# Four graph layers on one core: filler products on TensorE, one transposition bank, 512-wide work on gathered tiles, and a different first graph

## Chip, core and metric

The kernel runs on one core of a Trainium2 chip. Five engines work side by side, each through its own instructions in a fixed order: TensorE (PE; its weight loads are listed apart as PEld), VectorE (DVE), ScalarE (ACT), GpSimd (POOL) and SyncE (SP, which only issues transfers). The metric is the device time of one execution in microseconds; the number quoted for a kernel is the median of several runs.

## What is computed

Sixteen graphs of 1024 nodes with 64 features each pass through four layers. Every layer normalises the features, cuts them at zero, applies a graph operation and adds the result to its input.

```python
h = jnp.maximum(_layernorm(x, axis=-1), 0.0)
x = x + _L0_gnn_ref(h, adj, L0_gnn_W)        # adj @ h, then @ W.T
h = jnp.maximum(_layernorm(x, axis=-1), 0.0)
x = x + _L1_gnn_ref(h, adj, ...)             # two dense layers, adj @ m, a GRU cell
h = jnp.maximum(_layernorm(x, axis=-1), 0.0)
x = x + _L2_gnn_ref(h, adj, ...)             # Chebyshev: k0*h + k1*(A h) + k2*(2 A(A h) - h), @ weight
h = jnp.maximum(_layernorm(x, axis=-1), 0.0)
x = x + _L3_gnn_ref(h, adj, nodemask, ...)   # per node: quantiles over its kept neighbours, then an MLP
```

`adj` is dense in storage (1024 x 1024 float32 per graph, 4 MB) but has about nine non-zero entries in a row. The first three layers use it as a matrix. The last one needs, for each node, the list of its neighbours (with some of them dropped by a rule on the count), then for each of the 64 features the weighted sum of the 0.25, 0.5 and 0.75 quantiles over that list, a two-layer MLP and the node mask.

## The kernel before

**One program, seven chains.** The class `Fast` writes the work down as Python generators, each yielding operations one after another: `transposing` (load a graph's adjacency in eight blocks of 128 columns, 512 KB each, transpose them on PE, copy them out of PSUM by ACT into `AT` tiles), `coding` (from the signs of `AT`, bit codes of each node's neighbours, by small PE products), `listing` (from the codes, each node's list of up to 24 neighbours, on DVE), two `layering` chains (layers 0 to 2 and the last norm; one takes the even graphs, the other the odd ones), `gathering` (POOL fetches the neighbours' feature rows from a table in DRAM by indirect transfers of 128 rows each) and `quantiling` (sorting networks on DVE over the gathered rows; then `dense`, the weighting, the MLP and the output).

**The order is reckoned beforehand.** `Weave.run` takes the chains' next operations, gives each a cost from `Line.cost`, reckons when it could start, and fixes one order for each engine: earliest start first, within `SLACK` the chain with the lowest key. Keys put graph b's layers (b - 3) ahead of its transposing (b - 2.5), coding (b - 2), listing (b - 1.5), and gathering and sorting (b + 1). On the chip each engine runs its own order and waits where data are not there yet. So a wrong cost in `Line.cost` doesn't change what an instruction takes; it changes the order. Nearly all instructions are recorded at L301, in `Line`'s helper, and so are told apart by tile names.

**Buffers.** A chain asks for a tile by the name of its stock and blocks until one has been given back. Those that matter here: `pay` (4 tiles: a graph's features, its list and its notes, held from the load of x until its output is stored), `G` (2 tiles: gathered rows, 11 slots of 8 node tiles, 66 columns each), `net` (1 tile: the second buffer of the sorting network), `nodes` (3), `AT` (15), and the eight PSUM banks: two for transpositions (`tp`), one for codes (`bits`), two for `q` (quantiles, MLP and a few others), three for the layers (`fm`). Waits between engines go by regions of a tile: a gather into slot 2 of a G tile waits only for the readers of slot 2.

**Graph 0.** `layers` loads x, then for each of three layers normalises (`norm`) and multiplies by the `AT` tiles as they come. In `norm`, ACT makes the squares in eight pieces with an accumulated sum each, and eight relus with a scale; each relu is followed by what the caller passes as `then` (a pair of products per `AT` tile, or a transposition). At the end the graph's list and the normalised features are put into `pay`, and SP stores them to the tables from which POOL gathers.

**After gathering.** `quantiles` marks dropped neighbours with 1e30, runs the network `NETWORKS[11]` (28 minimum or maximum steps on 1 to 5 slots each), and weights the sorted slots. A step on k slots is cut by `parts(k)` into instructions of at most `few` slots, where `few` comes from `LONGEST` elements; a slot of a graph has 512. The nodes with more neighbours than these slots hold are gathered again at the end, in nine tiles (`MANY`), and their outputs are scattered over the earlier ones.

Of the kernel before, what the change touches and what calls it, by code (L numbers as in the profile page):

```python
# [16 lines left out]
AF = mybir.ActivationFunctionType  # L17
ALU = mybir.AluOpType
AX = mybir.AxisListType
# [3 lines left out]
P = 128  # L23
N = 1024
NT = N // P
C = 64
NB = 64
S = N // NB
# [18 lines left out]
SELF, COUNT, IDX, H, DROPS, MASK, TO, XS, W = ROW  # L47
# [57 lines left out]
LONGEST = 1024  # L105
# [180 lines left out]
class Line:  # L286
# [17 lines left out]
    def cost(self, method, out, reads, kwargs):  # L304
        n = max(a.free_size() for a in [out] + reads)
        extra = "accum_out" in kwargs
        if self.name == "DVE":
            fixed = {"match_replace": 0.27, "max": 0.16}.get(method, 0.155)
            return fixed + n / 960 + 0.08 * extra, 0.0
        if self.name == "ACT":  # L310
            scalars = sum(hasattr(kwargs.get(k), "ap") for k in ("bias", "scale"))
            return 0.225 + n / 1400 + 0.09 * scalars + 0.19 * extra, 0.0
        if self.name == "PE":
            if method == "transpose":
                return 0.12, 0.25
            n = out.free_size()
            if n == NB and mybir.dt.size(reads[0].dtype) == 2:
                return 0.12, 0.3
            pair = n == 512 and reads[0].shape[0] == P and out.shape[0] == C
            return (0.46 if pair else max(0.22, 0.06 + n / 545)), 0.3  # L320
        if self.name == "SP":
            return 0.4, 2.0 + out.nbytes() / 150e3
        return 1.33, 2.2


class Weave:
# [6 lines left out]
    def __init__(self, tc):  # L333
        self.tc = tc
        self.free, self.past, self.last, self.stocks, self.chains = {}, {}, {}, {}, []
        self.ends, self.time, self.free_pairs, self.count = {}, 0.0, set(), 0
        self.leash = None
        self.awaited, self.made = [], {}
# [4 lines left out]
    def give(self, name, t):  # L343
        self.stocks[name].append(t)
# [13 lines left out]
    def of_others(self, op, line):  # L358

        found = []  # L360
        for mine, kinds in ((op.reads, "w"), (op.writes, "wr")):
            for name, lo, hi, p0, p1 in mine:
                for (l, h, q0, q1, kind, other), made in self.made.get(name, {}).items():
                    if other is line and kind in kinds and l < hi and lo < h and q0 < p1 and p0 < q1:
                        found.append(made)
        return [max(found, key=lambda f: f[:2])] if found else []

    def note(self, op, start, ins):
        end = start + op.cost
        self.count += 1  # L370
        for mine, kind in ((op.reads, "r"), (op.writes, "w")):
            for name, lo, hi, p0, p1 in mine:
                past, made = self.past.setdefault(name, {}), self.made.setdefault(name, {})
                if kind == "w":
                    for e in [e for e in past if lo <= e[0] and e[1] <= hi and p0 <= e[2] and e[3] <= p1]:
                        del past[e], made[e]
                past[lo, hi, p0, p1, kind, op.line] = end + op.later
                made[lo, hi, p0, p1, kind, op.line] = end, self.count, ins
# [27 lines left out]
    def issue(self, op, start, of):  # L406

        line, ins = op.line, op.make()
        if line is self.leash[0]:


            done = [i for end, _, i in self.awaited if end <= start]
            self.awaited = self.awaited[len(done):]
            if done:
                self.after(ins, done[-1])
        self.free[line] = start + op.cost
        self.time = max(self.time, start + op.cost)
        if line is not self.leash[1]:
            self.awaited = sorted(self.awaited + self.of_others(op, self.leash[1]), key=lambda a: a[:2])
        self.note(op, start, ins)  # L420
        self.ends[ins.ins.name] = start + op.cost + op.later
        free = False
        for other in self.last.get(line, ()):
            self.behind(ins, other)
        if line in self.last:
            free = (ins.ins.name, self.last[line][0].ins.name) in self.free_pairs
        self.last[line] = [ins] + (self.last[line] if free else [])
        return ins

# [36 lines left out]
class Fast:  # L466
# [4 lines left out]
    def __init__(self, tc, half, whole, weights):  # L471
        self.tc, self.nc = tc, tc.nc
        (W0, W1, b1, W2, b2, Wih, bih, Whh, bhh, Wc, K, bc, M1, mb1, M2, mb2) = weights
        nc = self.nc
# [92 lines left out]
        self.G, self.D = Line("POOL", nc.gpsimd), Line("SP", nc.sync)  # L567
        self.take = {}
        weave.leash = None, None
# [5 lines left out]
        self.bank = banks[0]  # L575
        weave.stock("tp", banks[0:2])
# [58 lines left out]
    def listing(self, nodemask):  # L635
        V = self.V
        mf, mu8 = self.small("h1", (P, 512))[:, 0:P], self.small("h1")[:, P:2 * P].bitcast(U8)[:, 0:P]
        yield self.D.dma_start(mu8, nodemask.rearrange("b (t p) -> (b t) p", p=P))
        yield V.tensor_copy(mf, mu8)
        bank = yield "q"  # L640
        yield self.T.transpose(bank[:, 0:P], mf, self.ident)
        self.mask = self.small("mask", (P, P))
        yield V.tensor_copy(self.mask, bank[:, 0:P])
        self.weave.give("q", bank)
        for b in range(GRAPHS):
            yield float(b) + LIST_KEY
            yield from self.lists(b)
        yield float(GRAPHS) - RANK
        yield from self.longest()

    def coding(self):

        V, T, S = self.V, self.T, self.S
        for b in range(GRAPHS):
            yield float(b) + CODE_KEY
            bank = yield "bits"
# [188 lines left out]
    def transposing(self, adj):  # L845
# [5 lines left out]
        early = self.early  # L851

        def load(i):
            b, j = divmod(i, NT)
            blocks[i] = block = early.pop(0).rearrange("p (t m) -> p t m", m=P) if 2 <= i < NT else (yield "block")
            yield D.dma_start(block, adj[b, :, j * P:(j + 1) * P].rearrange("(t p) m -> p t m", p=P))
# [22 lines left out]
    def norm(self, w, h, X, then=None):  # L879
# [4 lines left out]
        yield V.tensor_scalar(st, st, -1.0 / C, None, op0=ALU.mult)  # L884
        sq = self.small(f"sq{w}", (P, C))
# [10 lines left out]
    def layers(self, w, b, x):  # L896
# [36 lines left out]
        yield from self.norm(w, h, X, into(bank, h))  # L933
# [25 lines left out]
        yield from self.norm(w, h, X, turn)  # L959
# [63 lines left out]
        yield from self.norm(w, h, X, into(bank, h))  # L1023
# [27 lines left out]
        aug = yield "wide"  # L1051
        for half in range(2):
            yield S.activation(aug[0:C, cols[half]], both[half * C:(half + 1) * C, :], AF.Copy)
        give("fm", both)
        bank = yield "fm"
        o = yield from by_node(bank, aug[0:C, :], self.wca, self.bcr)
        give("wide", aug)
        yield V.tensor_add(X, X, o)
        give("fm", bank)

# [12 lines left out]
        yield from self.norm(w, pay[:, :, H:H + C], X)  # L1073
# [873 lines left out]
```

## Time and profile before

| | |
|---|---|
| median of 9 runs | 2264.45 us (2258.52 to 2275.44) |
| the profiled execution | 2274.12 us, span 2272.3 us |
| mean granted clock of PE | 0.757 |
| first gather issued / last gather issued | 161.0 / 2227.9 us |
| graph tables stored by SP (graphs 0, 1, 2, 3, 4) | 155.7, 255.7, 372.9, 476.5, 594.1 us |
| PE, DVE, ACT, POOL busy from 300 to 1700 us | 1186.7, 1041.3, 810.5, 1045.1 of 1400 us |
| granted clock of PE from 300 to 1700 us | 0.80 |
| adjacency block, SP to landing | 512 KB, 4.5 us |

The profile is of one execution. An engine's busy time is the union of its instructions. A row such as `DVE G L301 ... x97 | 117.5, 1221 | 1.0` gives a group of like instructions: count, busy us together, mean ns of one, and idle time ahead of them. In a timeline row the first two numbers are start and length in us, and the bracket gives how long the engine stood idle just before and which work ended that. In a row of waits, "A <- B: total, times, longest" says how long A stood until B released it. The granted clock is the share of its full clock that PE was given; the trace knows only the values 1 and 0.5, and a stretch's number is their mean.

### The profile page before, as it was taken

Reading aid. Unit: us, or ns where it says so; the run is one execution under the profiler, and the core shown is the slowest. Engines: PE = TensorE matmul, PEld = TensorE weight load, DVE = VectorE, ACT = ScalarE, POOL = GpSimd, SP = SyncE. Lnnn points to the kernel's source line nnn. Section 1 sums busy time; section 2 is a strip of 40 time slices with the busy share of each in tenths; the row PEclk is TensorE's granted clock in tenths of the full one; section 3 lists DMA queues with packets and bytes.
Section 4 is the critical chain, followed back from the end, with each engine's and each line's share of the span. In section 5 each row is a group of like instructions: output and inputs, shape, how many; then the busy total and the mean of one; then the engine's idle time right before and its main releaser. Section 6 shows DMA issues by size and latency. Waiting matters only on the chain. (4 is left out here: it accounts for less than half of the span.)

```text
span 2272.3 us, 24102 instructions
## 1 busy us (share of the span) xinstructions
PE 1662.2 (73%) x7024; PEld 762.7 (34%) x7024; DVE 1551.6 (68%) x3675; ACT 1095.3 (48%) x3002; POOL 1570.6 (69%) x1441
## 2 busy tenths in 40 slices
PE   5869697888887888797988897888888762332303
PEld 2333333343434343343343343343333321111302
DVE  1515277695968695958687867777776889939745
ACT  4555546564756565656565646465555531011000
POOL 2017776777777787777677777576777677877773
PEclk9778788868887878787888778787768675555555
DMA  4123434352636252535243434344252413121110
GB/s 115 47 53 83 75 79 75 64 93 44 93 73 94 53 94 53 77 69 79 58 80 68 67 63 76 66 77 69 53 78 62 35 30 36 27 29 24 33 26 11
DMA packets 246841, 141.00 MB, mean 62 GB/s; under 512 B 76048, under 2 KB 223952, under 8 KB 246704
## 3 DMA queue, kind: packets, MB, share of 16 engines
q0 software_dynamic: 46096, 48.62, 18.5%
q1 hardware_dynamic: 199824, 90.21, 16.4%
q8 instruction: 59, 0.97, 0.2%
q10 hardware_dynamic: 784, 0.57, 0.1%
q14 instruction: 78, 0.64, 0.1%
HBM read 120.12 MB, written 19.17 MB: 61 GB/s over the span
## 5 line engine op out<-in xcount | busy, mean ns | idle before, releaser
L622 POOL DMA_INDIRECT G<-table,pay x1402 | 1538.8, 1098 | 655.3 <-issue 337.6
L301 PE MATMUL bank<-AT,nodes 128*64 128x512 f32 x2048 | 621.7, 691 | 48.1 <-ACT nodes L301 23.2
L301 PE MATMUL bank<-G,c 128*128 128x512 f32 (+3 forms) x382 | 190.0, 617 | 169.7 <-DVE G L301 169.7
L301 PEld LDWEIGHTS bank<-AT,nodes 128*64 128x64 f32 x2048 | 162.4, 155 | 358.5 <-issue 235.9
L301 PE MATMUL bank<-c,block 128*128 128x128 f32 x976 | 215.4, 347 | 35.3 <-DMA block<-in_adj 28.4
L301 ACT ACTIVATE sq<-pay,st 128x64 f32<-128x64 f32 x512 | 177.7, 347 | 96.4 <-DVE st L301 82.5
L301 ACT ACTIVATE AT<-bank 128x512 f32<-128x512 f32 x256 | 150.5, 589 | 121.5 <-PE bank L301 120.4
L301 PEld LDWEIGHTS bank<-c,block 128*128 128x128 f32 x976 | 142.2, 176 | 171.9 <-issue 125.0
L301 DVE TENSOR_TENSOR G<-G 128x1024 f32<-128x1024 f32 (+7 forms) x215 | 187.5, 903 | 2.2
L301 ACT ACTIVATE nodes<-pay,off,ri 128x64 f32<-128x64 f32 x384 | 153.6, 429 | 23.1 <-DVE off L301 22.8
L301 ACT ACTIVATE wide<-bank 64x512 f32<-64x512 f32 x128 | 75.7, 591 | 180.6 <-PE bank L301 179.6
L301 PEld LDWEIGHTS bank<-G,c 128*128 128x128 f32 x382 | 69.5, 226 | 275.7 <-issue 142.7
L301 ACT ACTIVATE G<-G,coef 128x64 f32<-128x64 f32 x384 | 95.2, 336 | 128.0 <-DVE coef L301 128.0
L301 DVE TENSOR_TENSOR net<-G 128x1024 f32<-128x1024 f32 (+7 forms) x140 | 140.5, 1033 | 3.1 <-PE bank L301 2.0
L301 ACT ACTIVATE there<-AT 128x1024 f16<-128x1024 f32 x128 | 132.4, 1045 | 0.3
L301 PE MATMUL bank<-c,nodes 128*64 128x128 f32 x128 | 50.8, 400 | 86.3 <-ACT nodes L301 85.9
L301 DVE TENSOR_TENSOR G<-net 128x512 f32<-128x512 f32 (+12 forms) x123 | 109.4, 938 | 1.4
L301 DVE TENSOR_TENSOR G<-G,net 128x1024 f32<-128x1024 f32 (+5 forms) x113 | 104.3, 960 | 1.4
L301 DVE SCALAR_TENSOR_TENSOR G<-bad,G 128x1024 f32<-128x1024 f32 (+3 forms) x89 | 102.6, 1202 | 0.0
L301 PE MATMUL bank<-wide,wg 64*64 64x512 f32 (+1 forms) x192 | 101.4, 609 | 1.1 <-ACT wide L301 1.0
L301 DVE MAX8 L<-cand 128x8 f16<-128x103 f16 x384 | 92.3, 263 | 8.8
L301 DVE TENSOR_TENSOR more<-more,top 128x64 f32<-128x64 f32 x80 | 17.7, 221 | 116.4 <-ACT sq L301 116.4
(188 smaller groups left out, 2375.1 us busy)
## 6 DMA issues: line engine op xcount, KB each, us to landing
block<-in_adj SPq DMA_DIRECT2D x122, 512.0 KB, 4.5
G<-table,pay POOLq DMA_INDIRECT x1402, 2.7
rows<-pay SPq DMA_DIRECT2D x16, 632.0 KB, 9.6
table<-pay SPq DMA_DIRECT2D x16, 264.0 KB, 5.0
pay<-in_x SPq DMA_DIRECT2D x16, 256.0 KB, 4.1
out<-yo SPq DMA_DIRECT2D x16, 256.0 KB, 2.8
G<-in_adj SPq DMA_DIRECT2D x6, 512.0 KB, 9.7
c<-in_half ACTq DMA_DIRECT2D x1, 246.0 KB, 7.7
```

The lines of the kernel that those rows point to most:

```text
L301: return Op(self, lambda: f(*args, **kwargs), writes, reads, cost, later)
L622: return self.nc.gpsimd.indirect_dma_start(out=out, out_offset=None, in_=table, in_offset=bass.IndirectOffsetOnAxis(ap=at, axis=0))
```

## The change

- **Fillers.** `Weave.fill`: before an operation of PE is placed, the gap that the reckoned order leaves ahead of it is taken. If it is over 0.22 us and layers are still being placed, and the reckoned PE work of the last 3.4 us is under half of that, products of a constant (`ones16`, 128 x 512 float16) are put in front, for at most 0.7 of the gap at 0.22 us each. They write a bank that nobody reads.
- **Banks.** That bank is the first of the two that were in `tp`; one is left for transpositions.
- **Costs.** `Line.cost` has other costs for PE (a half of a pair of 512 columns 0.27 in place of 0.46, others to match, a small f16 product 0.05 in place of 0.12), for DVE's `match_replace` and `max`, and one for transfers on any queue.
- **Width.** `LONGEST` is 512 in place of 1024: at most one slot of a graph in an instruction.
- **First graph.** The first blocks' loads with odd number go through ACT's queue, the others through SP's. The node mask is cast and transposed only once graph 0's codes are there. Coding starts when graph 0's first aggregation is through. Graph 0's norms make the squares and the scaled relu on DVE over all eight pieces at once.
- **All graphs.** At the end of `layers` the list and the notes are put into `pay` ahead of the last product with the weights, not behind it.
- **Taken out.** The code around `leash`, which was set to `None, None`.

```diff
-LONGEST = 1024
+LONGEST = 512
+WINDOW = 3.4
+DENSITY = 0.5
+SPARE = 0.7
+FILL = 0.22
...
     def cost(self, method, out, reads, kwargs):
+        if method == "dma_start":
+            return 0.4, 2.0 + out.nbytes() / 150e3
...
-            fixed = {"match_replace": 0.27, "max": 0.16}.get(method, 0.155)
+            fixed = {"match_replace": 0.145, "max": 0.155}.get(method, 0.155)
...
             if method == "transpose":
-                return 0.12, 0.25
+                return 0.125, 0.25
             n = out.free_size()
             if n == NB and mybir.dt.size(reads[0].dtype) == 2:
-                return 0.12, 0.3
+                return 0.05, 0.3
             pair = n == 512 and reads[0].shape[0] == P and out.shape[0] == C
-            return (0.46 if pair else max(0.22, 0.06 + n / 545)), 0.3
-        if self.name == "SP":
-            return 0.4, 2.0 + out.nbytes() / 150e3
+            return (0.27 if pair else max(0.15, 0.06 + n / 1100)), 0.3
         return 1.33, 2.2
...
     def issue(self, op, start, of):
-        line, ins = op.line, op.make()
-        if line is self.leash[0]:
...
+        line = op.line
+        if line is self.filled:
+            self.fill(start, op.cost)
+        ins = op.make()
...
+    def fill(self, start, cost):
+        line = self.filled
+        gap = start - self.free.get(line, 0.0)
+        self.recent = [(a, c) for a, c in self.recent if a > start - WINDOW]
+        if gap > FILL and any(c["gen"].__name__ == "layering" for c in self.chains):
+            lacking = DENSITY * WINDOW - sum(c for _, c in self.recent)
+            for _ in range(int(min(lacking, SPARE * gap) / FILL)):
+                ins = self.filler()
+                for other in self.last.get(line, ()):
+                    self.behind(ins, other)
+                self.last[line] = [ins]
+                self.recent.append((start, FILL))
+        self.recent.append((start, cost))
...
-        self.bank = banks[0]
-        weave.stock("tp", banks[0:2])
+        self.bank = spare = banks[0]
+        weave.filler = lambda: nc.tensor.matmul(spare, self.ones16[:, 0:P], self.ones16, start=True, stop=True)
+        weave.stock("tp", banks[1:2])
...
         yield self.D.dma_start(mu8, nodemask.rearrange("b (t p) -> (b t) p", p=P))
+        yield lambda: 0 in self.coded
         yield V.tensor_copy(mf, mu8)
...
             yield float(b) + CODE_KEY
+            yield lambda: self.turns > 0
             bank = yield "bits"
...
-            yield D.dma_start(block, adj[b, :, j * P:(j + 1) * P].rearrange("(t p) m -> p t m", p=P))
+            queue = self.A if i % 2 and i < NT else D
+            yield queue.dma_start(block, adj[b, :, j * P:(j + 1) * P].rearrange("(t p) m -> p t m", p=P))
...
-    def norm(self, w, h, X, then=None):
+    def norm(self, w, h, X, then=None, early=False):
...
+        if early:
+            yield V.tensor_add(h, X, st[:, :, None].to_broadcast([P, NT, C]))
+            square = yield "nodes"
+            yield V.tensor_mul(square, h, h)
+            yield V.tensor_reduce(va, square, axis=AX.X, op=ALU.add)
+            self.weave.give("nodes", square)
+            yield S.activation(sd, va, AF.Sqrt, bias=self.eps, scale=1.0 / C)
+            yield V.reciprocal(ri, sd)
+            yield V.scalar_tensor_tensor(h, h, 0.0, ri[:, :, None].to_broadcast([P, NT, C]), op0=ALU.max, op1=ALU.mult)
+            for t in range(NT):
+                if then:
+                    yield from then(t)
+            return
...
-        yield from self.norm(w, pay[:, :, H:H + C], X)
+        yield from self.norm(w, pay[:, :, H:H + C], X, early=b == 0)
```

More of the change, by code (lines that the diff above doesn't have):

```diff
@@ L335, in __init__ @@
         self.free, self.past, self.last, self.stocks, self.chains = {}, {}, {}, {}, []
-        self.ends, self.time, self.free_pairs, self.count = {}, 0.0, set(), 0
-        self.leash = None
-        self.awaited, self.made = [], {}
+        self.ends, self.time, self.free_pairs = {}, 0.0, set()
+        self.filled, self.recent = None, []
     def stock(self, name, tiles):
@@ L356, in ready, with note @@
         return t
[L358 to L368, printed above, removed]
+    def note(self, op, start):
         end = start + op.cost
-        self.count += 1
         for mine, kind in ((op.reads, "r"), (op.writes, "w")):
             for name, lo, hi, p0, p1 in mine:
-                past, made = self.past.setdefault(name, {}), self.made.setdefault(name, {})
+                past = self.past.setdefault(name, {})
                 if kind == "w":
                     for e in [e for e in past if lo <= e[0] and e[1] <= hi and p0 <= e[2] and e[3] <= p1]:
-                        del past[e], made[e]
+                        del past[e]
                 past[lo, hi, p0, p1, kind, op.line] = end + op.later
-                made[lo, hi, p0, p1, kind, op.line] = end, self.count, ins
     def advance(self, chain):
@@ L406, in issue @@
     def issue(self, op, start, of):
-        line, ins = op.line, op.make()
-        if line is self.leash[0]:
[L412 to L415, printed above, removed]
+        line = op.line
+        if line is self.filled:
+            self.fill(start, op.cost)
+        ins = op.make()
         self.free[line] = start + op.cost
         self.time = max(self.time, start + op.cost)
-        if line is not self.leash[1]:
-            self.awaited = sorted(self.awaited + self.of_others(op, self.leash[1]), key=lambda a: a[:2])
-        self.note(op, start, ins)
+        self.note(op, start)
         self.ends[ins.ins.name] = start + op.cost + op.later
@@ L567, in __init__ @@
         self.G, self.D = Line("POOL", nc.gpsimd), Line("SP", nc.sync)
+        self.A = self.S
         self.take = {}
-        weave.leash = None, None
+        weave.filled = self.T
         def stock(name, count, shape, dtype=F32):
@@ L932, in layers @@
         bank = yield "fm"
-        yield from self.norm(w, h, X, into(bank, h))
+        yield from self.norm(w, h, X, into(bank, h), early=b == 0)
         self.turns += 1
@@ L958, in turn @@
                 give("fm", turned_h[-1])
-        yield from self.norm(w, h, X, turn)
+        yield from self.norm(w, h, X, turn, early=b == 0)
         aug = yield "wide"
@@ L1022, in layers @@
         bank = yield "fm"
-        yield from self.norm(w, h, X, into(bank, h))
+        yield from self.norm(w, h, X, into(bank, h), early=b == 0)
         wide = yield "wide"
@@ L1050, in layers @@
         give("nodes", h)
[L1051 to L1059, printed above, removed]
         yield lambda: b in self.listed
@@ L1072, in layers @@
         give("notes", notes)
-        yield from self.norm(w, pay[:, :, H:H + C], X)
+        aug = yield "wide"
+        for half in range(2):
+            yield S.activation(aug[0:C, cols[half]], both[half * C:(half + 1) * C, :], AF.Copy)
+        give("fm", both)
+        bank = yield "fm"
+        o = yield from by_node(bank, aug[0:C, :], self.wca, self.bcr)
+        give("wide", aug)
+        yield V.tensor_add(X, X, o)
+        give("fm", bank)
+        yield from self.norm(w, pay[:, :, H:H + C], X, early=b == 0)
         table = self.table[b * STRIDE:b * STRIDE + N, :].rearrange("(t p) c -> p t c", p=P)
```

## The prediction

> **What bounds the kernel now.** I read the page's engine totals first, then the gathers by tile.
>
> ```profile
> PE 1662.2 (73%) x7024; PEld 762.7 (34%) x7024; DVE 1551.6 (68%) x3675; ACT 1095.3 (48%) x3002; POOL 1570.6 (69%) x1441
> PEclk9778788868887878787888778787768675555555
> ...
> POOL G L622 <- DMA table<-pay: 145.1, 2, 143.6
> ...
> L622 POOL DMA_INDIRECT G<-table,pay x1402: 938/945/1997, 161.0 to 2227.9; - x176
> ```
>
> No engine is full by its share, yet POOL (GpSimd) sets the time. It waits 143.6 us for the first table, gathers from 161.0 to 2227.9, and hardly stops. The 1402 gathers, 9 row gathers and 9 scatters are busy 1538.8 + 10.8 + 9.3 = 1558.9 us. The pauses after 161.0 are 655.3 + 2.7 + 30.1 - 143.6 = 544.5 us: in the instruction records, 1419 of them with a median of 0.305 (433 us) plus 112 us beyond that in 22 long ones, of which 27 lie between the last scatters. So 161.0 + 1558.9 + 544.5 = 2264.4, and some 8 us follow. Three terms can shrink: the 161 us ahead, the time that gathers lose above their floor of 0.945 (1558.9 - 1420 x 0.945 = 217 us), and about 85 us of long pauses inside the loop.
>
> The second term comes from DVE (VectorE):
>
> ```profile
> 1069.39 1.98 POOL L622 DMA_INDIRECT G<-table,pay  x1 [0.30 <-ACT nodes L301]
> ...
> 1069.34 1.22 DVE L301 TENSOR_TENSOR net<-G,net 128x1024 f32<-128x1024 f32 x1
> 1070.59 1.23 DVE L301 TENSOR_TENSOR net<-G 128x1024 f32<-128x1024 f32 x1
> ```
>
> The gather took 1.98 us beside two 1.22 us operations on the sorting tiles. Over all records, the 257 gathers that met no DVE instruction average 0.944; the 411 that mostly met a 1024-wide G or net operation average 1.347 (+0.403, 166 us together); the 108 that met a 512-wide one 1.126 (+0.182).
>
> The third term: graph b+2's gathers need the G buffer that graph b's sort still reads.
>
> ```profile
> 1099.39 0.96 POOL L622 DMA_INDIRECT G<-table,pay  x1 [11.26 <-PE bank L301]
> ...
> 1097.83 0.23 DVE L301 TENSOR_TENSOR more<-more,top 128x64 f32<-128x64 f32 x1 [10.63 <-ACT sq L301]
> ...
> 428.86 0.38 SPq L628 DMA_DIRECT2D out<-yo  x1
> 429.30 0.58 SPq L301 DMA_DIRECT2D pay<-in_x  x1
> ```
>
> While POOL waits 11.26, DVE itself stands 10.63 in its fixed order behind an ACT (ScalarE) read. Sorting starts 13 to 51 us after its gathers end (graphs 1 to 14), though DVE idles 18 to 41 us per graph through graph 12. The last two lines show the pay ring: graph 4's x is loaded when graph 0's output leaves. From graph 3 to graph 13 the period is (1673.3 - 496.5) / 10 = 117.7 us, of which 80 x (0.944 + 0.305 + 0.15 lost) = 112 is gathering.
>
> **First graph (the 161 us).**
>
> ```profile
> 23.80 0.23 DVE L301 CAST h<-h 128x128 f32<-128x128 uint8 x1 [11.18 <-DMA h<-in_nodemask]
> 24.08 0.18 PEld L301 LDWEIGHTS bank<-c,h 128*128 128x128 f32 x1 [10.10 <-DVE h L301]
> 25.23 0.44 ACT L301 ACTIVATE nodes<-pay,off,ri 128x64 f32<-128x64 f32 x1 [10.21 <-DVE off L301]
> ```
>
> The node mask is queued on SP behind eight 512 KB loads, and DVE, PE (TensorE) and ACT all stand about 10 us behind its cast. The change makes cast and transposition wait for the first code. Transposing then runs from 13.3, where block 0 is there. With one bank, four transpositions (0.66), the ACT copy (0.60) and two hand-overs (some 0.2) follow each other: 1.46 a half, 1.6 with the product that does not fit under the copy; 16 halves end at 13.3 + 25.6 = 39, the last pair at 40 in place of 51: -11. The DMA engines are full from 8 to 22 us (268 to 302 GB/s), so the second queue moves that end little. Four loads on ACT hold it 4 x 2.3 us (SP's median there) from 5.3 to 14.5, just when the first copy is due; at 3.6 each, 5 us are lost. The weights that PE's set-up awaits until 11.6 were issued ahead of them. Range -14 to -6.
>
> Norms of graph 0: before, 8 x 0.47 of squares on ACT, then 8 relus between products. After: four 512-wide DVE operations (four by 0.69), root 0.30, reciprocal 0.20, gaps 0.2, that is 3.5. Second norm with its transpositions: from 16.6 us (51.0 to 67.6) to about 10.2, counting copy 1.2, product 2.0, add 0.7, sums 0.9, 3.5, eight transpositions 1.3, copy 0.6: -6.4. Third: 6.8 to 4.4, and relus no longer between the products: -5.4. Last: 144.4 to 155.6 becomes 4.6: -6.6. Together -18.4. Pay's six small DVE operations (143.69 to 144.41) go under PE's products: -0.7. Coding (8 copies of 1.045 on ACT, 128 small products) now follows the first aggregation instead of lying in it, and returns +4. Half-clock products between 67 and 79 (four in 3.67 us, against about 0.6 each at full clock) shrink by 4 if fillers hold the clock, 0 if not. Sum -30, bounds -42 to -12. POOL gets it all only if tables 1 and 2 (stored at 255.7 and 372.9, POOL then waited 1.5 and 11.6) move as far; I take **-28**.
>
> **Width 512.** Per graph the network has 66 slot operations: 40 instructions before, 66 after; mask adds 5, weighting 3: 34 more. Over all, 555 operations of 1.22 become 1110 of 0.686 (+84 us DVE, 5.1 a graph), hidden under the idle above. If that cover is gone, it goes into the G wait in full, +84. Gathers that meet them: 411 x 1.12 = 461; at +0.182 they lose 84 in place of 166 (-82), at a loss proportional to length (+0.226) 104 (-62), at an unchanged +0.403, +20. I take **-65**, near the proportional end, range -82 to +20.
>
> The Trainium skill (SBUF — State Buffer, "Who interferes with whom") speaks against this: a two-input DVE operation blocks only a GpSimd instruction that reads SBUF, and descriptor writing is inferred untouched. By it, if descriptor writing is what these gathers do, width would gain 0; by the rows, 65. The rows decide.
>
> **New costs, order, fillers.** The modelled cost of a 128x512 pair half goes from 0.46 to 0.27. Measured: 621.7 / 2048 = 0.30 busy each, so 0.27 is nearer; DVE's and ACT's places in the order shift everywhere. No row prices that. Bounds: all long loop pauses vanish (-85), or DVE's stalls stay and the 84 above appears. I take **-25**, a third: the dearest stall, "more" behind "sq", is 109.8 us in 300 to 1700, and PE would be faster. The clock there is 0.80, so 40% of the time is at half. Fillers (0.22 each modelled) can be at most 15% idle x 117.7 x 0.7 / 0.22 = 56 a graph. They wait for nothing; behind one stand only PE's own products, delayed by 0.22 to 0.44. Recovering half of the lost clock takes about 11% off PE's 1187 us there.
>
> The skill (TensorE: Matmul & The Clock Gate, "What's actually happening") says the clock halves after an idle window of about 3.4 us. Here spans at half clock last up to 65 us although PE is 81% busy in those of the loop; so half a window of density need not hold it. By the rule all -4 and more would come; by the row perhaps none.
>
> One bank fewer: 16 hand-overs of 0.7 a graph, 0 to 11 us of PE, taken as 2 and covered by the 24 us between graph 4's table (594.0) and its first gather (618.1). The deleted leash code matches no engine: 0. Tail: two or three more 0.15 us operations, 0.3.
>
> **Sum.** 2274.1 (the profiled execution's own time; span 2272.3) - 28 - 65 - 25 = 2156. It ran 9.7 above the median of 2264.45, so the forecast is **2146**, own range 2090 to 2200.
>
> **Rivals.**
> *DVE takes it back.* The sort of b must end before b+2's second slot is gathered; cheaper gathers only wait longer. For: sorting always starts late. Against: DVE idles. Then only the first graph counts: 2264 - 28 = 2236.
> *POOL runs free.* Pauses gone, shorter meeting, -30 - 75 - 75: 2084. For: DVE and PE have idle time; against: in-order queues never lost all of it.
> *Nothing carries.* Start gain eaten by table 2, width by DVE: 2264.
> *Slower: the pay ring.* Graph 4: load 429.3, table 594.0 (165), gather 618.1 (slack 24) to 729.3 (111), output 904.8 (175); four graphs in 476. If PE runs at the old clock under costs for the full one, its products arrive late and ACT and DVE stand behind them. To lose 7 us in spite of -28, the loop must cost 35 / 14 = 2.5 a graph, 10 a ring of four: layers and sort, now 165 + 175 = 340, must first use up the slack beyond the table's 5 us of landing (19) and the shorter gather (4), so they decide from +33 on. Fillers (56 x 0.22 to 0.44 = 12 to 25 a graph) and bank hand-overs (11) over some 1.5 graphs of layers, with 10 us of new stalls, give about +60: (60 - 23) / 4 = 9 a graph, 14 x 9 - 28 = +98: 2362. Against: most fillers fall where PE idles.
>
> **Numbers.** Forecast 0.45, DVE takes it back 0.25, free 0.12, nothing 0.05, slower 0.13. About 0.3% (7 us) is what a measurement can tell from no change: faster 0.82, same 0.05, slower 0.13. The range 2085 to 2258 leaves out the slower case, nothing, and a little of the free one.
>
> **What would show it.** First gather near 131; no DVE wait on the mask; gather mean near 1.05; period near 112; loop clock above 0.85; no 1024-wide G operation. Wrong: first gather near 131 but a period still of 117 (DVE takes it back), or a gap between table and gather that is gone with PE over 90% busy (pay ring).

## The result: 2377.01 us, slower, and the profile after

The changed kernel takes 2377.01 us (median of 10 runs, 2365.01 to 2384.4) against 2264.29 us for the kernel before (31 runs): ratio 1.0495, interval 1.0472 to 1.0517. The profiled execution took 2377.39 us, span 2375.5. The forecast was 2146.

From the page after, the engine totals, the granted clock in 40 slices, and three groups (count, busy us, mean ns, idle time ahead):

```profile
PE 1703.8 (72%) x7692; PEld 775.1 (33%) x7692; DVE 1603.4 (67%) x4253; ACT 1074.7 (45%) x2905; POOL 1413.0 (59%) x1441
...
PEclk9989788989798788887978888898988785555555
...
L624 POOL DMA_INDIRECT G<-table,pay x1402 | 1383.7, 987 | 915.9 <-issue 335.8
L305 PE MATMUL bank<-AT,nodes 128*64 128x512 f32 x2048 | 569.8, 670 | 134.4 <-ACT nodes L305 127.9
...
L577 PE MATMUL bank<-ones 128*128 128x512 f16 x668 | 231.0, 484 | 9.1 <-DVE wg L546 9.1
```

The first two groups on the page before:

```profile
L622 POOL DMA_INDIRECT G<-table,pay x1402 | 1538.8, 1098 | 655.3 <-issue 337.6
L301 PE MATMUL bank<-AT,nodes 128*64 128x512 f32 x2048 | 621.7, 691 | 48.1 <-ACT nodes L301 23.2
```

Read the gathers' line first. POOL (GpSimd) gathers faster than before, 987 ns in the mean instead of 1098, yet stands idle longer ahead of the gathers, 915.9 us instead of 655.3. Its account, made as in the prediction, closes again: first gather at 161.6; all 1420 indirect transfers busy 1401.3 us (before 1558.9, so -157.5); pauses of 0.305 between them 433 us as before; long pauses 372 us beyond that (before 112, so +260). -157.5 + 260 = +102.5, and the last gather moves by just that, from 2227.9 to 2330.4. The last line of the page after shows 668 fillers, and the loop's clock rose (0.80 to 0.85 from 300 to 1700 us). So both things that the change was to improve did improve, and the time came back as pauses of POOL.

The waits name who holds it ("A <- B: total, times, longest"):

```profile
POOL G L624 <- DVE net L305: 290.9, 15, 30.5
...
DVE of_h L305 <- ACT wide L305: 153.1, 17, 14.6
...
DVE pay L305 <- PE bank L305: 100.3, 28, 25.6
```

and in the trace before:

```profile
DVE pay L301 <- PE bank L301: 39.6, 13, 12.2
...
POOL G L622 <- DVE net L301: 31.3, 6, 11.6
DVE of_h L301 <- ACT wide L301: 31.1, 4, 10.6
```

From graph 3 on POOL waits some 20 us ahead of nearly every graph's gathers for DVE's sort (`net`) of the graph two before, 290.9 us in all; it was 31.3 before. And DVE itself stands behind the layers: for `of_h` (a step of the GRU cell) 153.1 us (31.1 before), for `pay` 100.3 (39.6 before). Only the very first gather waits for a table: graph 4's is stored at 591.2 and its first gather comes at 656.2. What is late is the G ring, that is, the two G tiles in turn: graph b+2 is gathered into the tile that graph b's sort still reads.

One graph's tangle of waits, in the timeline (start, length, and in the bracket the idle time ahead and its releaser):

```profile
748.23 9.31 PE L305 MATMUL bank<-AT,nodes 128*64 128x512 f32 x32 [0.47 <-ACT nodes L305]
...
757.60 1.21 ACT L305 ACTIVATE wide<-bank 64x512 f32<-64x512 f32 x2 [9.14 <-PE bank L305]
...
749.52 2.53 DVE L305 TENSOR_TENSOR G<-net,G 128x512 f32<-128x512 f32 x4
760.84 0.74 DVE L305 SCALAR_TENSOR_TENSOR of_h<-bank,bhn,wide 64x512 f32<-64x512 f32 x1 [8.79 <-ACT wide L305]
761.61 1.29 DVE L305 TENSOR_TENSOR G<-net,G 128x512 f32<-128x512 f32 x2
...
780.33 1.15 POOL L624 DMA_INDIRECT G<-table,pay  x1 [20.58 <-DVE net L305]
```

An aggregation on PE is 16 products (32 records) and takes 9.31 us here. The order has DVE do four sorting operations beside it and then go to `of_h`, which needs the aggregation's result. DVE stands 8.79 us with a sort half done, and POOL, which waits for that sort, stands 20.58. The new cost table prices those 16 products at 16 x 0.27 = 4.3 us. DVE begins to stand in the same way at 878.4, 1002.2, 1127.5 and 1253.4, once a graph.

The first graph gained nothing (first gather at 161.6, before 161.0), and the timeline of its first microseconds shows the first cause:

```profile
9.39 8.45 ACTq L305 DMA_DIRECT2D G<-in_adj  x3
...
17.86 1.28 ACT L305 ACT_TABLE_LOAD   x1 [17.86 <-DMA G<-in_adj]
19.16 0.30 ACT L305 ACTIVATE sd<-va,eps 128x8 f32<-128x8 f32 x1
19.49 0.20 DVE L305 RECIPROCAL ri<-sd 128x8 f32<-128x8 f32 x1 [9.41 <-ACT sd L305]
20.74 3.14 PE L577 MATMUL bank<-ones 128*128 128x512 f16 x7 [9.08 <-DVE wg L546]
...
23.68 1.06 PE L305 MATMUL bank<-c,block 128*128 128x128 f32 x4
```

Three of the loads that moved to ACT occupy its queue from 9.39 to 17.86; the root behind them, DVE's reciprocal and copy behind that, and seven fillers ahead of the first transposition put it at 23.68, where it was at 13.27 before.

### The profile page after: what moved, and what is told of

The parts are those of the page before. It is cut to its first block, busy times and chain, and to the rows that moved or that the text cites. A ratio compares the mean times of both kernels' runs of the same rounds, so it can differ in the third digit from the quotient of the medians.

```text
span 2375.5 us, 25989 instructions
## 1 busy us (share of the span) xinstructions
PE 1703.8 (72%) x7692; PEld 775.1 (33%) x7692; DVE 1603.4 (67%) x4253; ACT 1074.7 (45%) x2905; POOL 1413.0 (59%) x1441
## 5 line engine op out<-in xcount | busy, mean ns | idle before, releaser
L624 POOL DMA_INDIRECT G<-table,pay x1402 | 1383.7, 987 | 915.9 <-issue 335.8
L305 PE MATMUL bank<-AT,nodes 128*64 128x512 f32 x2048 | 569.8, 670 | 134.4 <-ACT nodes L305 127.9
L305 PE MATMUL bank<-c,block 128*128 128x128 f32 x976 | 190.7, 311 | 69.9 <-ACT AT L305 53.2
L577 PE MATMUL bank<-ones 128*128 128x512 f16 x668 | 231.0, 484 | 9.1 <-DVE wg L546 9.1
L305 DVE TENSOR_TENSOR G<-G 128x512 f32<-128x512 f32 (+3 forms) x313 | 197.7, 674 | 2.3
L305 DVE TENSOR_TENSOR net<-G 128x512 f32<-128x512 f32 (+6 forms) x240 | 148.8, 671 | 1.6 <-PE bank L305 1.4
L305 DVE SCALAR_TENSOR_TENSOR of_h<-bank,bhn,wide 64x512 f32<-64x512 f32 x32 | 23.8, 744 | 172.8 <-ACT wide L305 153.1
L305 DVE TENSOR_TENSOR G<-net 128x512 f32<-128x512 f32 (+7 forms) x189 | 115.6, 669 | 0.9
L305 DVE TENSOR_TENSOR G<-G,net 128x512 f32<-128x512 f32 (+3 forms) x177 | 111.0, 678 | 0.7
L577 PEld LDWEIGHTS <-ones 128*128 128x128 f16 x668 | 76.0, 119 | 108.3 <-issue 80.7
L305 DVE SCALAR_TENSOR_TENSOR G<-bad,G 128x512 f32<-128x512 f32 (+1 forms) x176 | 110.1, 693 | 0.0
```

Source lines behind the costliest of these rows:

```text
L305: return Op(self, lambda: f(*args, **kwargs), writes, reads, cost, later)
L577: weave.filler = lambda: nc.tensor.matmul(spare, self.ones16[:, 0:P], self.ones16, start=True, stop=True)
L624: return self.nc.gpsimd.indirect_dma_start(out=out, out_offset=None, in_=table, in_offset=bass.IndirectOffsetOnAxis(ap=at, axis=0))
```

## The experiments

Three theories. **A**: the lowered PE costs make the order plan layer products at half their length, so that DVE is sent to wait for them while its sort is open. **B**: the fillers (and the single bank) take PE's time. **C**: sorting 512 wide makes DVE the bound by itself.

In four of the five sessions the kernel before took 3394 to 3400 us and not 2264, and in the fifth 2252.14 us (2243.65 to 2263.37). In the long sessions PE, ACT and DVE stand still for part of each graph's gathers (shown under `after_again`). Ratios from there are ratios to 3395 and not to 2264, and I use them only where a second set, with the gathers taken out, agrees. The expectations in us of the runs there were written for 2264 and cannot be applied; only their ratios can.

### One part back, one part alone (long sessions)

The changed kernel with the old cost table:

```diff
-            fixed = {"match_replace": 0.145, "max": 0.155}.get(method, 0.155)
+            fixed = {"match_replace": 0.27, "max": 0.16}.get(method, 0.155)
...
-                return 0.125, 0.25
+                return 0.12, 0.25
...
-                return 0.05, 0.3
+                return 0.12, 0.3
...
-            return (0.27 if pair else max(0.15, 0.06 + n / 1100)), 0.3
+            return (0.46 if pair else max(0.22, 0.06 + n / 545)), 0.3
```

> The changed kernel with the cost table of the kernel before (a pair half 0.46 again, and so on); fillers, one transposition bank, width 512 and the first graph stay. Theory A (the new PE costs are half of what a float32 product takes, so the order lets DVE stand behind layer products that come late, and the sort starts late): the pause before each graph's gathers (20 us) mostly goes, the sort's lag behind the gathers falls from 35 to 91 us to 10 to 50 as before, and the time falls from 2377 to 2200 to 2270. Theory B (fillers take PE's time): fewer gaps are reckoned, so fewer fillers, and the time falls too, but the lag stays above 35 us unless fillers fall to near none. Theory C (512-wide sorting makes DVE the bound): no change beyond 20 us, 2357 to 2390.

Measured 3521.88 us, 1.0365 (1.0327 to 1.0402). Run again in another session:

> The changed kernel with the cost table of the kernel before, again. Theory A: the sort's lag behind the gathers falls to 10 to 50 us, gathers average 0.99, the time falls from 2377 to 2200 to 2270. Theory B: with as many fillers as in the first session (456) it stays above 2300. Theory C: 2357 to 2390.

3530.61 us, 1.0392 (1.0370 to 1.0414).

The kernel before with the new table alone (the same four lines, the other way round):

> The kernel before with the new cost table alone. Theory A: this alone makes the loop slow, 2264 rises to 2340 or more, with pauses before each graph's gathers and sorting that starts over 35 us late. Theories B and C: nothing of theirs is in it, so it stays within 2230 to 2300.

Measured 3664.9 us, 1.0788 (1.0750 to 1.0826), and again:

> The kernel before with the new cost table alone, again, since in the first session the kernel before itself took 3396 us in place of 2264 and engines stood for 50 us at a time without a cause in the program. Theory A (the costs make the order wrong): 2264 rises to 2340 or more, with pauses before each graph's gathers and sorting that starts over 35 us late. Theories B (fillers) and C (width): it stays within 2230 to 2300.

3671.19 us, 1.0800 (1.0780 to 1.0821).

The changed kernel without fillers:

```diff
-DENSITY = 0.5
+DENSITY = 0.0
```

> The changed kernel with DENSITY 0, so no filler is placed; costs and everything else as changed. Theory B (668 fillers take 231 us of PE and hold up real products): 2377 falls to below 2300. Theory A (costs): the order of the real instructions stays, so the time moves by less than 30 us, to 2350 to 2400; the granted clock falls back from 0.87 towards 0.80 in the loop.

Measured 3685.77 us, 1.0843 (1.0796 to 1.0889).

And with the old width:

```diff
-LONGEST = 512
+LONGEST = 1024
```

> The changed kernel with LONGEST 1024 again. Theory C (width): DVE has 84 us less to do and the sort ends earlier, 2377 falls to 2300 or below, though gathers go back from 0.987 to about 1.10 on average. Theory A: the gathers were not the bound any more, so their longer time fills the pauses, and the time moves by less than 40 us in either direction.

Measured 3542.81 us, 1.0428 (1.0386 to 1.0471).

The changed kernel itself, with no edit:

> The changed kernel itself, unaltered, as the anchor in the sessions of the study, where the kernel before takes about 3396 us and not 2264 us. If a session gives 2264 us for the kernel before, it must give about 2377 us (1.05). If it gives 3396 us: theory A (the lowered PE costs make the order put DVE's sorting late) expects it clearly above the changed kernel with the old costs (1.037 to 1.039), at 1.07 to 1.12; theory B (the fillers take PE's time) expects it near that kernel with the old costs, 1.03 to 1.05, since both hold fillers; theory C (sorting 512 wide makes DVE the bound) expects it above the variant with LONGEST 1024 (1.043) by 2% or more.

Measured 3670.83 us, 1.0819 (1.0747 to 1.0891). Its windows (length, busy time of each engine with its count, then clock, DMA share, GB/s) and one row of the timeline show what is different in these sessions:

```profile
560.00:590.00 30.00, 26.82 (x99) 10.08 (x97) 20.12 (x45) 14.81 (x37) 14.38 (x14) 0.97 0.32 85
610.00:660.00 50.00, 0.00 (x0) 0.00 (x0) 0.00 (x0) 0.00 (x0) 32.23 (x35) 0.50 0.17 24
```

```profile
661.34 1.39 ACT L305 ACTIVATE wide<-bank,k 64x512 f32<-64x512 f32 x2 [65.17 <-remote]
```

From 610 to 660 POOL issues 35 gathers and no other compute engine moves; ACT is let go after 65.17 us by something that the profile does not know. The loop in the result's trace of the same kernel has no such stretch.

The kernel before with the new width alone:

```diff
-LONGEST = 1024
+LONGEST = 512
```

> The kernel before with LONGEST 512 alone. Where the kernel before takes 2264 us: theories A and B expect the gathers' gain undisturbed, 130 to 160 us of gathering less on GpSimd and 5 us more sorting a graph on DVE, so 2180 to 2240 us, ratio 0.96 to 0.99. Theory C expects 2270 to 2330 us, ratio 1.00 to 1.03, with GpSimd waiting for DVE's net ahead of each graph. Where the kernel before takes 3396 us, with engines standing still while a graph is gathered: A and B expect 0.97 to 1.00, C 1.02 or more.

Measured 3485.27 us, 1.0256 (1.0191 to 1.0321).

And with the fillers and one transposition bank alone (`fill` as in the change):

```diff
-        line, ins = op.line, op.make()
+        line = op.line
+        if line is self.filled:
+            self.fill(start, op.cost)
+        ins = op.make()
...
-        self.bank = banks[0]
-        weave.stock("tp", banks[0:2])
+        self.bank = spare = banks[0]
+        weave.filler = lambda: nc.tensor.matmul(spare, self.ones16[:, 0:P], self.ones16, start=True, stop=True)
+        weave.stock("tp", banks[1:2])
```

> The kernel before with the fillers and one bank for transpositions alone, at the old costs. Theory A expects little of it: 0.98 to 1.01, with a granted clock higher than the kernel before has in its loop. Theory B expects 1.03 or more, since some 600 fillers of 0.35 us and the single bank lie on PE's path.

Measured 3448.97 us, 1.0159 (1.0094 to 1.0223), between what A and B expected.

So in these sessions the cost table alone does to the kernel before what the whole change does (1.079 and 1.082), and putting it back takes 149 us off the changed kernel (3670.83 - 3521.88). Taking the fillers out gains nothing, against B. The width costs something from either side (91 us alone, 128 us in the changed kernel), for C as a lesser part. `b_w512` missed the range that A and B share (0.97 to 1.00) and hit C's. But the standing engines make every graph wait out its own gathers, so none of this is proof for the sessions at 2264 us.

The changed kernel with all block loads on SP:

```diff
-            queue = self.A if i % 2 and i < NT else D
-            yield queue.dma_start(block, adj[b, :, j * P:(j + 1) * P].rearrange("(t p) m -> p t m", p=P))
+            yield D.dma_start(block, adj[b, :, j * P:(j + 1) * P].rearrange("(t p) m -> p t m", p=P))
```

> The changed kernel with all loads of adjacency blocks on SP. Every theory on the loop expects the loop unchanged. In the first graph the ACT queue is no longer held from 9 to 18 us by three loads: the first transposition then starts near 14 us and not at 23.7, and the first gather comes 5 to 10 us earlier than the changed kernel's 161.6 us; the total 3 to 10 us below the changed kernel's. If the loads and not ACT's queue set the start, nothing changes.

Measured 3666.35 us, 1.0790 (1.0720 to 1.0859), in the total not to be told from `after_again`. The timeline has the start as expected:

```profile
9.59 0.30 ACT L305 ACTIVATE sd<-va,eps 128x8 f32<-128x8 f32 x1 [3.01 <-DVE va L305]
...
11.24 3.15 PE L577 MATMUL bank<-ones 128*128 128x512 f16 x7 [1.52 <-DVE wg L546]
...
14.18 1.06 PE L305 MATMUL bank<-c,block 128*128 128x128 f32 x4
```

The root comes at 9.59 and the first transposition at 14.18, 10.2 us earlier than in `after_again` (24.39 in that run), and the first gather at 155.6 in place of 164.5. ACT's queue held the start; the transfers themselves did not.

### The order by itself: fills in place of the gathers

To get rid of the standing engines and of the gathers' stretching at once, all but the first gather of each group give way to fills on POOL, which with their short pauses take 1.28 to 1.29 us a row (a gather that meets nothing takes 0.944 + 0.305 = 1.25); slots, waits and the written order stay. Some of the fills stand a few places ahead of their turn, in all kernels of the set alike.

```diff
+            if row is not None:
+                self.nc.gpsimd.memset(row, 0.0)
+                self.nc.gpsimd.memset(row, 0.0)
+                return self.nc.gpsimd.memset(out, 0.0)
             return self.nc.gpsimd.indirect_dma_start(
...
-                                  reads)
+                                  reads, row=G[:, k + 1, 0 if k else 1:T, :] if k + t else None)
```

> The kernel before, with all but the first gather of each group of gathers left out: three fills of the tile's row on GpSimd stand in their place, some 1.2 us together by the one fill of the trace (2.76 us for 3168 elements), so that the pace stays near the 1.25 us of an undisturbed gather and no data are gathered. It computes no right output. If the gathers are what holds the engines still in the study's sessions, the stalls are gone and the time falls from 3394 us to 2000 to 2250 us, a graph every 105 to 115 us; if not, it stays near 3400 us. Measured against the three others of this set, it gives the price of the order alone, with the width of the sorting's pieces and the gathers' stretching taken out of GpSimd's pace.

Measured 2203.1 us (2188.01 to 2214.14) in a session where the kernel before took 3395.56. So the gathers, and not the session alone, are what the engines stand still for, and the set can be read beside 2264 us. With the other three:

> The changed kernel with the same fills in place of the gathers, which leaves the gathered data out in the same way. Theory A (the lowered costs make an order in which DVE's sorting stands behind layer products) expects it 80 to 200 us slower than the kernel before so treated, GpSimd waiting for DVE's net in both but longer here. If the order costs nothing by itself and the loss of the changed kernel lay in the gathers, the two are within 30 us.

> The kernel before with the changed cost table alone, and the same fills in place of the gathers. Theory A expects it slower than the kernel before so treated by 60 us or more; theories B (fillers) and C (512 wide) expect it within 20 us, as it has neither fillers nor narrower pieces.

> The changed kernel with the old cost table, and the same fills in place of the gathers. Theory A expects it faster than the changed kernel so treated by 60 us or more, and within 30 us of the kernel before so treated. Theories B and C expect it at the changed kernel's time, within 20 us.

Measured: changed kernel 2353.78 (2350.93 to 2359.95), before with the new costs 2467.72 (2464.46 to 2474.86), changed with the old costs 2192.29 (2174.45 to 2194.45). As ratios to the kernel before of that session (3395.56): p_before 0.6482 (0.6451 to 0.6513), p_after 0.6944 (0.6923 to 0.6965), p_newcost 0.7280 (0.7257 to 0.7303), p_oldcost 0.6450 (0.6417 to 0.6483). The waits of the four, in that order:

```profile
POOL G L623 <- DVE net L301: 64.0, 14, 20.5
...
DVE of_h L301 <- ACT wide L301: 27.6, 4, 8.6
```

```profile
POOL G L628 <- DVE net L305: 232.7, 13, 31.1
...
DVE of_h L305 <- ACT wide L305: 145.7, 17, 14.4
```

```profile
POOL G L626 <- DVE net L301: 329.0, 15, 46.4
...
DVE of_h L301 <- ACT wide L301: 163.6, 17, 12.2
```

```profile
POOL G L625 <- DVE net L305: 94.7, 14, 20.5
...
DVE of_h L305 <- ACT wide L305: 26.9, 5, 17.4
```

Compare the second row of each with the result's traces: 31.1 before, 153.1 after. The wait follows the cost table: about 27 with the old one, in either kernel, about 150 with the new one, in either kernel. With DVE's wait for `pay` (40.2, 92.9, 136.6 and 65.1 in the same order) it changes by 147 us in the changed kernel and by 232 in the kernel before, most of what the time changes by. POOL's wait for `net` moves with them; in three of the four it has a second row (36.3, 25.3 and 40.0 in `p_before`, `p_after` and `p_oldcost`), so it is 100, 258, 329 and 135 us in all. With the new table graphs come every 122.6 us (`p_after`, from graph 3 to 13) and 131.3 (`p_newcost`), with the old one every 115.5 (`p_before`) and 114.7 (`p_oldcost`); the result's own traces have 117.7 and 123.6. Theory A is shown: the table costs 161 us in the changed kernel and 265 us in the kernel before. B and C expected `p_oldcost` at `p_after`'s time, and it is 161 us below. The old table also makes the order place fewer fillers (456 in `p_oldcost`, 668 in `p_after`), but that is not the reason: `p_newcost` and `p_before` have none, and there the table costs more.

Which entry of the table? Only the two product costs put back:

```diff
-            return (0.27 if pair else max(0.15, 0.06 + n / 1100)), 0.3
+            return (0.46 if pair else max(0.22, 0.06 + n / 545)), 0.3
```

> The changed kernel with fills in place of the gathers (gathered data left out, as before) and only the two lowered TensorE product costs put back: 0.46 for a product of the aggregation, 0.06 + n/545 for the others. All other new costs stay. If the product costs are the cause (each float32 product counted at half its time), it takes 2180 to 2220 us, as with the whole old table (2192 us), against 2354 us with the new one. If DVE's own lowered cost (0.145 for match_replace) or the transpositions' matter as much, it stays above 2250 us.

Measured 2196.14 us (2177.67 to 2202.99), ratio 0.9769 (0.9732 to 0.9806) to the kernel before of the last session (2252.14). Its waits:

```profile
POOL G L625 <- DVE net L305: 83.5, 13, 18.7
...
DVE of_h L305 <- ACT wide L305: 22.9, 4, 18.0
```

That is p_oldcost again, in a session of the other kind, so the fills make the set independent of the session as far as these two tell. The product costs are the whole loss of the table; its other new entries together are worth nothing that can be measured. Which of the two product entries weighs more was not tried.

With 0.61 for a product of the aggregation, near its measured mean, the old table otherwise, and the fills:

```diff
-            return (0.46 if pair else max(0.22, 0.06 + n / 545)), 0.3
+            return (0.61 if pair else max(0.22, 0.06 + n / 545)), 0.3
```

> The changed kernel with fills in place of the gathers (gathered data left out) and the old cost table, but 0.61 for a product of the aggregation, which is what the trace gives for one with both of its records (621.7 us over 1024 products). If the order is the better the nearer the costs are to the chip's, 2150 to 2195 us; if the old 0.46 was only tuned by trial, 2195 to 2300 us.

Measured 2195.64 us (2185.04 to 2213.55), 0.9771 (0.9706 to 0.9835): no better than 0.46. It lies at the edge between the two expectations, so this run does not decide whether costs nearer to the chip's gain; it shows that between 0.46 and 0.61 the order hardly cares, where 0.27 and its like cost 161 us.

The changed kernel with the fills, the old table and pieces 1024 wide:

```diff
-LONGEST = 512
+LONGEST = 1024
```

> The changed kernel with fills in place of the gathers (gathered data left out), the old cost table and LONGEST 1024. GpSimd's pace is the same, so what is left is DVE's side of the width: 5 us less sorting a graph in larger pieces. If DVE stands on the path, 2100 to 2170 us, against 2192 us at 512; if not, 2185 to 2200 us.

Measured 2154.31 us (2149.98 to 2161.61), 0.9567 (0.9534 to 0.9599): 42 us below p_pair in the same session. So DVE stands on the path, and 512-wide pieces, 84 us more work for DVE in all, cost about 40 us there.

### Pauses between the gathers

The changed kernel with the old table, all loads on SP and all its gathers, with four fills (2.1 us) ahead of every eight gathers:

```diff
+            if row is not None:
+                for _ in range(4):
+                    fill = self.nc.gpsimd.memset(row, 0.0)
...
-                                  reads)
+                                  reads, row=None if t else G[:, k + 1, :, :])
```

> The changed kernel with the old cost table and all block loads on SP, which gathers all data, and with four fills of the row (2.1 us) on GpSimd ahead of every eight gathers. In these sessions PE, ACT and DVE stand still some 25 us into each run of gathers and move again when GpSimd pauses. If any pause of GpSimd sets them free, the stalls go and the time falls from about 3515 us to 2300 to 2700 us. If only the end of the gathers does, it rises by the fills, 16 times 22 us, to 3600 to 3900 us.

Measured 2482.23 us, 1.1028 (1.0992 to 1.1064), but in the last session, where the kernel before took 2252.14 and the long stretches of standing engines were missing. So the question that it was made for stays open: what POOL's run of gathers withholds from the other engines in the long sessions, and why only there, was not found. The run is of use otherwise; its group and one wait:

```profile
L631 POOL DMA_INDIRECT G<-table,pay x1402 | 1404.7, 1002 | 550.7 <-issue 366.3
...
POOL G L631 <- DVE net L305: 0.3, 1, 0.3
```

With the real gathers and the old costs POOL waits 0.3 us for DVE in all: a graph comes every 127.7 us, which is POOL's own work (80 gathers of 1.00 + 0.305 are 104.4, forty fills of 0.54 are 21.5, and hand-overs). Without the fills DVE would be next at 115 or so, as in `p_oldcost`; I estimate 2082 (2482 less the 400 us of its 880 fills) at the least and about 2215 (2192 + 23, the 23 from 2377 - 2354) at the most. The changed kernel with the old costs and no fills was not run in a session at 2252 us, and no run that gathers all its data beat the kernel before.

## Why the prediction was wrong

With the set's medians the whole difference can be written down: +162 for the costs (2192.3 to 2353.8), +38 for 512-wide pieces on DVE (2154 to 2192), -49 for all the rest of the change at equal costs and width (2203 to 2154), and -38 because the real gathers stretch less (they add 61 to the kernel before, 2264 - 2203, and 23 to the changed one, 2377 - 2354). The sum is +113, the measured difference, as it must be: each term is the step from one run to the next. Only the terms say something, and they depend on the order of the steps: taken first, on the kernel before, the costs are +265 and the rest of the change -114. They also join runs of several sessions, and the medians of the set stand in runs that spread by 9 to 26 us, so each term has such a play.

**New costs, order, fillers: -25. This is the step that failed.** The prediction read "621.7 / 2048 = 0.30 busy each, so 0.27 is nearer". The 2048 are records, and each of the 1024 float32 products of the aggregation leaves two. Per product it is 621.7 / 1024 = 0.61 us in the mean; so the old 0.46 was below that and the new 0.27 less than half of it. In the aggregation at 748.23 the records start two by two, and the next two follow after 0.853 us at half clock and 0.429 at full clock: 0.43 a product at the best, close to the old price. The entry for the other products, 0.06 + n / 1100, has the same slip: 0.53 for 512 columns, where two records of `wide,w` take 1.07. The count was in reach: 16 graphs, four aggregations, 8 blocks, two halves are 1024. The bounds set for this step (-85 to +84) held the loss of the sort on DVE but not one of an order that plans with half lengths, and the costs alone measured +162; fillers and the single bank are in the -49, not told apart. The Trainium skill (FP8 and Floating Point Precision, "TensorE Precision Notes") says that a true float32 product makes four passes through the array. The trace fits that in time: a product by itself in the first graph takes PE from 29.26 to 30.27 us, 1.0, at full clock, where a float16 filler of the same 512 columns follows the one before by 0.216; in a dense run two such products take 0.858 together, four times 0.216, as if they ran side by side. That two records stand for one product is shown by the count above.

**Width 512: -65.** The gathers did gain, and more than forecast: 539 gathers that mostly met a 512-wide operation on the sorting tiles lost 0.084 each, not 0.182, and the gathers' mean fell to 0.987, below the 1.05 that was named. How much of that is the width and how much the new order is not told apart; in `a_break`, as wide but with the old costs, some 540 such gathers lost 0.113. What was mis-sized is what it is worth. The prediction took POOL's time for the kernel's. In `p_before` POOL's work with its short pauses is 1815 us in place of 1985, 170 less, but the kernel is only 61 us below 2264: the pauses over 0.6 us grow from 118 to 225. And the cover under which the 84 us of extra DVE work was put was thin: `p_w1024` prices it at 40. Together -38 + 38: nothing, in place of -65. The Trainium skill (SBUF — State Buffer, "Who interferes with whom") infers that descriptor writing is untouched by such two-input operations; the prediction asked whether that covers these gathers. It does not cover them as a whole: they lose 0.40 us beside a 1024-wide operation before, and 0.084 beside a 512-wide one after. Which part of a gather is held up, the descriptors or the reading of its row numbers from `pay`, no run here shows.

**First graph: -28, measured 0.** "Four loads on ACT hold it from 5.3 to 14.5" was too early: they hold it to 17.86, and the queue's setup ahead of the root cost 9 us (a_sp). "16 halves end at 39, 1.6 each" priced a block's two halves with one product under the copy; at twice the product's time, and with a filler between the halves, a block takes 4.26 us and the aggregation ends near 60, not 40. The norms were shorter, as expected, and gave those 10 us back. The costs weighed here too: with the old ones the first gather is at 148.9 (p_oldcost) against 162.9 (p_after).

**Rivals.** "DVE takes it back" named the ring that did it (the very first gather apart): POOL waits for `net` of the graph two before. It was priced at "only waits longer", 2236, because DVE's standing time was taken as given. The pay ring, which gave the number nearest to the result (2362), had the premise right, "its products arrive late and ACT and DVE stand behind them", but not for the reason given: the clock rose, and tables now lie some 60 us before their gathers. So its price, close to the result, was luck.

**Signs.** Met: no 1024-wide G operation, no DVE wait on the mask, clock 0.85 in the loop ("above 0.85" was named). Missed: first gather (131 forecast, 161.6), gather mean (1.05, 0.987), period (112, 123.6). Of fillers the forecast allowed up to 56 a graph; there are 42 (668 / 16).

## What to carry

A cost table that an order is planned with is code on the critical path: check every entry as busy time divided by instructions of the program, not by records of the trace. An underpriced producer is dear, since the engine that waits for it holds up whatever else stands in its queue; pricing the same product at 0.61 in place of 0.46 changed nothing; at 0.27, with the other products halved likewise, it cost 161 us. And time saved on an engine that is only the last to wait is worth what the next one in the ring allows: take that time away in one run before pricing a change to it.

## What the hardware showed unexpectedly

Three 512 KB transfers issued by ACT hold its queue for 8.45 us, so that the instruction behind waits until 17.86. A 128-row gather slows by 0.40 us beside a 1024-wide two-input operation of DVE, but by 0.084 beside a 512-wide one in the changed kernel and 0.113 in `a_break`, less than the half that the width would give; the kernel before has 0.18 for its 512-wide ones, so the width is not the whole of it. A float32 product of 512 columns leaves two records in the trace. And in the long sessions PE, ACT and DVE all stood still while POOL went on gathering: in `after_again` there are 29 such stretches of over 8 us, the longest 54, 590 us in all (0.00 us of work from 610 to 660). With fills on POOL in the gathers' place they were gone; the cause is open.
